# Layer 3 of a four-layer image kernel: GpSimd's additions kept back by a one-column copy, VectorE's taps divided anew among three units

## Chip, cores and metric

The kernel runs on one core of a Trainium2 chip. The metric is the device time of one execution in microseconds. Three executions of the kernel before took 12,790.3, 12,794.5 and 12,797.0 us.

## What is computed

The input is a float32 image batch of 4 x 48 x 256 x 256. Four layers follow each other; each normalises in groups, applies its function and adds the result to its input. Layers 0 and 3 are feed-forward layers with a spectral filter, layers 1 and 2 are scans over rows and columns. The change touches layer 3 alone:

```python
y = einsum('oc,bchw->bohw', w_in, x)          # 48 -> 288 channels
f = rfft2(8x8 patches of y) * fft_mask
y = irfft2(f)
y = conv 3x3, one filter per channel (w_dw)   # 288 channels
x1, x2 = split(y, 2)                          # 144 + 144
g = gelu(x1) * x2
out = einsum('oc,bchw->bohw', w_out, g)       # 144 -> 48
```

In layer 3 this function is applied to the normalised image, and the image is added to it.

## The kernel before

Layer 3 works on two pairs of images. A pair's 256 rows are cut into strips of 8 rows (RB); after the 32 strips of a pair comes one short step, the tail, for the last row. That makes 66 steps, 64 of them full strips.

The 288 channels of the 3x3 convolution are in three groups of image buffers: z_a0 and z_a1 (the halves x1 and x2 of the first 128 channels, for one image of the pair), z_b0 and z_b1 (the same for the other image), and z_m, which holds the 16 channels that are left over, for both images and both halves. The nine taps of the convolution are computed in three ways at once:

- **TensorE** does all of a0 and a1, and the lower half of the rows of b0 and b1, as products with small diagonal matrices (L1173, L1189). 288 such products make a *unit*. A step has three units: a0, a1 and b.
- **VectorE** does the upper half of the rows of b0 and b1. begin (L1232) has ScalarE write tap 0, and eight further taps follow, each a scalar_tensor_tensor over 128x1024 that reads an image and an accumulator in SBUF (L1237). The eight wait in the list due, and together hands them out one at a time while a unit runs. After the eighth tap of b0 comes ScalarE's gelu (L1239), after that of b1 a product of the two accumulators (L1241).
- **ScalarE and GpSimd** do z_m. narrow lays out 18 pieces of work in the list coming: nine taps times two halves of the rows. For a tap, ScalarE writes a product into part (L1263; three buffers), and GpSimd adds part to acc_m (L1264, 128x512). Tap 0 is ScalarE's alone (L1260). product takes one piece from the list, and its calls stand at chosen places of the step.

A step runs like this. Pixels of a0 are made from the spectra (products pp, L1133, and copies to z_a); then the second half of the spectra of this step (pz, L1095, with VectorE's L1098 and L1103) lies between the two pixel products of b0; then unit a0 runs. In it stands the gate of the previous step's z_m: gate_few finishes the list coming, then narrow_gate computes gelu on ScalarE (L1282, into a buffer gl) and the product on VectorE (L1285). Then the pixels of a1 are made and copied by VectorE (L1053, z_a), those of z_m follow, the previous step's output products run (po, L1300 and L1312), VectorE adds the input to them (L1324) and SyncE stores them. Then comes unit a1, with its gates (L1220) at the end. Then come the waves of the next step (pf, L1074), the pixels of b1 and the first half of the next step's spectra (L1095, L1098). Then unit b runs; at its end lower_gate has ScalarE compute a gelu (L1199) and VectorE two products (L1201).

All these PSUM tiles (pd, pp, pz, po, pt, pf) come from one pool of four buffers with the one tag w. The buffers gl come from a pool with two, as do the output rows xo.

The order on TensorE, VectorE, ScalarE and SyncE is that of the code. GpSimd is not in that list, and its order is left to the scheduler that builds the program:

```python
FIXED = {mybir.EngineType.PE, mybir.EngineType.DVE, mybir.EngineType.Activation}
...
st.enter_context(tc.manual_schedule(engines=FIXED | {mybir.EngineType.SP}))
```

The taps are handed out by this line of together, where t runs over the nine taps of a unit and k % 3 is 0 in unit a0:

```python
if due and (t in (0, 1, 3, 4, 6) or t == 7 and k % 3 == 0):
    due.pop(0)[1]()
```

Of the kernel before, what the change touches and what calls it, by code (L numbers as in the profile page):

```python
# [9 lines left out]
F32 = mybir.dt.float32  # L10
AF = mybir.ActivationFunctionType
ALU = mybir.AluOpType
# [21 lines left out]
class Net:  # L34
# [903 lines left out]
    def layer3(self, x, scs):  # L938
# [6 lines left out]
        nc, tc, W, H, NQ, HD = self.nc, self.tc, self.W, self.H, self.NQ, HID3  # L945
        NM, NR, WP, R2 = 128, HID3 - 128, W + 2, MM // W
        steps = [(p, s) for p in range(self.NP) for s in range(H // RB + 1)]
        tail = lambda step: step[1] == H // RB
        odd = lambda step: steps.index(step) % 2
        with ExitStack() as st:  # L950
            pool = lambda name, bufs, **k: st.enter_context(tc.tile_pool(name=name, bufs=bufs, **k))
            wp, inp, wz = pool("w3", 1), pool("in3", 1), pool("z3", 1)
            io, mid = pool("io3", 2), pool("mid3", 1)
            ps_w = pool("ps3w", 4, space=PSUM)
            st.enter_context(tc.manual_schedule(engines=FIXED | {mybir.EngineType.SP}))
            HR = RB // 2
# [79 lines left out]
            gated = {g: wz.tile([128, 4, MM], F32, name=f"g_{g}", tag=f"g_{g}") for g in "ab"}  # L1036
# [159 lines left out]
            def lower_gate(pds):  # L1196
                gl = io.tile([128, 2, MM], F32, name="gl", tag="gl")
                x1, x2 = (pd.rearrange("p k r w -> p k (r w)") for pd in pds)
                nc.scalar.activation(gl, x1, AF.Gelu)  # L1199
                for l in range(2):  # L1200
                    nc.vector.tensor_tensor(  # L1201
                        gated["b"][64:128, 2 * l : 2 * l + 2], gl[64 * l : 64 * l + 64],
                        x2[64 - 64 * l : 128 - 64 * l], ALU.mult,
                    )
# [5 lines left out]
            def curve(step, x1):  # L1210
                gl = io.tile([128, 2, MM], F32, name="gl", tag="gl")
                x1 = flat(step, x1)
                gl = gl[0 : x1.shape[0], 0 : x1.shape[1], 0 : x1.shape[2]]
                nc.scalar.activation(gl, x1, AF.Gelu)  # L1214
                return gl

            def gate(step, img, k0, gl, x2):
                to, x2 = gated[img], flat(step, x2)
                n, k, m = x2.shape
                nc.vector.tensor_tensor(to[0:n, k0 : k0 + k, 0:m], gl, x2, ALU.mult)  # L1220
# [3 lines left out]
            whole, full, due, begun = {}, set(), [], {}  # L1224
# [18 lines left out]

                due.extend(((step, half), lambda t=t: tap(t)) for t in range(1, 9))

            few, coming, curved = {}, [], [None]

            def narrow(step):


                n, rows = (64, 1) if tail(step) else (128, HR)
                at = lambda t: zt["m"][0:n, t // 3 : t // 3 + rows, t % 3 : t % 3 + W]
                acc = mid.tile([128, HR, W], F32, name="acc_m", tag="acc_m")
                few[step] = acc
                acc = acc[0:n, 0:rows]
                half = lambda ap, r: ap[:, R2 * r : min(R2 * r + R2, rows)]

                def tap(t, r):
                    if t == 0:
                        nc.scalar.activation(half(acc, r), half(at(0), r), AF.Identity, bias=none[0:n], scale=wd[0:n, 2, 0:1])  # L1260
                        return
                    part = mid.tile([128, R2, W], F32, name="part", tag="part", bufs=3)[0:n, 0 : min(R2, rows)]
                    nc.scalar.activation(part, half(at(t), r), AF.Identity, bias=none[0:n], scale=wd[0:n, 2, t : t + 1])  # L1263
                    nc.gpsimd.tensor_tensor(half(acc, r), half(acc, r), part, ALU.add)  # L1264

                halves = range(1 if tail(step) else 2)
                coming.extend(lambda t=t, r=r: tap(t, r) for t in range(9) for r in halves)

            def product(last=False):
                while coming:  # L1270
                    coming.pop(0)()
                    if not last:
                        return

            def narrow_gate(step, j0):
                if j0 == 0:
                    curved[0] = io.tile([128, HR, W], F32, name="gl", tag="gl")
                gl, acc = curved[0], few[step]
                for j0 in (j0,) if j0 == 0 or not tail(step) else ():
                    x1, x2 = slice(32 * j0, 32 * j0 + 32), slice(32 * j0 + 32, 32 * j0 + 64)  # L1280
                    rows = 1 if tail(step) else HR
                    nc.scalar.activation(gl[x2, 0:rows], acc[x1, 0:rows], AF.Gelu)  # L1282
                    for j in range(1 if tail(step) else 2):
                        to, r = slice(32 * (j0 + j), 32 * (j0 + j) + 32), slice(R2 * j, min(R2 * j + R2, rows))
                        nc.vector.tensor_tensor(acc[to, r], gl[x2, r], acc[x2, r], ALU.mult)  # L1285
# [58 lines left out]
            def unit(l, step, img):  # L1344


                n, blocks = steps.index(step), (2 * l, 2 * l + 1)
                pd = None
                if img == "b":
                    if not tail(step):  # L1350
                        if l == 0:
                            both[:] = [ps_w.tile([128, 2, R2, W], F32, name="pd", tag="w") for _ in range(2)]
                        yield from lower_taps(l, blocks, both)
                else:
                    pd = ps_w.tile([128, 2, R2, W], F32, name="pd", tag="w")
                    yield from taps(step, img, int(img[1]), blocks, pd)
                if img == "a0":
                    waiting[l] = curve(step, pd)
                    return
                assert n == 0 or steps[n - 1] in out  # L1360
                if img == "a1":
                    gate(step, "a", 2 * l, waiting[l], pd)
                elif l and not tail(step):
                    lower_gate(both)

            def together(k, aside):


                going = [unit(l, *units[l][k]) for l in range(2)]
                for t in range(9):  # L1370
                    for g in list(going):
                        if next(g, None) is None:
                            going.remove(g)
                    if t in aside:
                        aside[t]()
                    if due and (t in (0, 1, 3, 4, 6) or t == 7 and k % 3 == 0):
                        due.pop(0)[1]()
                for g in going:
                    assert next(g, None) is None
# [14 lines left out]
            def ready(n):  # L1394

                if fresh(n):
                    state["u"] = normed(steps[n])
# [15 lines left out]
            def spectra(n, k, part=slice(None)):  # L1413
                if fresh(n):
                    for q0, m in (cuts_rest if k else cuts)[part]:
                        spectrum(state["xf"], k, q0, m)

            def lower(n, half, q0, eng):
                if q0 == 0 and n:
                    drain(steps[n - 1], half)  # L1420
                pixels(steps[n], f"b{half}", q0, eng)
                if q0:
                    begin(steps[n], half)

            def gate_few(n, j0):
                if n >= 0:
                    product(True)
                    narrow_gate(steps[n], j0)

# [10 lines left out]
            for n, step in enumerate(steps):  # L1440
                pixels(step, "a0", 0, "AA")
                pixels(step, "a0", 8, "AA")
                product()
                spectra(n, 1, slice(0, 1))
                lower(n, 0, 0, "AA")
                spectra(n, 1, slice(1, 3))
                lower(n, 0, 8, "AA")
                spectra(n, 1, slice(3, None))
                product()
                gates = {4: lambda: gate_few(n - 1, 0), 6: lambda: gate_few(n - 1, 2)}  # L1450
                together(3 * n, {0: product, 1: product} | gates)

                pixels(step, "a1", 0, "DD")
                pixels(step, "a1", 8, "DD")
                pixels_rest(step, "AA")
                store(n - 1)
                narrow(step)
                if fresh(n + 2):
                    fetch(steps[n + 2])
                turn(n + 1, "AA")  # L1460
                together(3 * n + 1, {t: product for t in (0, 2, 3, 5, 6, 8)})

                wave(n + 1, "AA")
                product()
                lower(n, 1, 0, "AA")
                product()
                lower(n, 1, 8, "AA")
                product()
                spectra(n + 1, 0)
                together(3 * n + 2, {t: product for t in (0, 1, 5, 7, 8)} | {3: lambda: ready(n + 2)})  # L1470
            gate_few(S - 1, 0)
            gate_few(S - 1, 2)
            store(S - 1)
# [118 lines left out]
```

## Time and profile before

| | us |
|---|---|
| median of three runs | 12,794.5 |
| the profiled execution, its own time | 12,789.3 |
| its span | 12,787.5 |
| PE busy in the span | 11,859.6 (93%) |
| DVE busy | 7,870.3 (62%) |
| ACT busy | 4,692.9 (37%) |
| POOL busy | 3,177.0 (25%) |
| mean granted TensorE clock | 0.983 |

Layer 3 takes the last third of the span. In the stretch from 8700 to 12300 us, 3600 us long, the engines were busy for: PE 3286.87, DVE 2863.53, ACT 2270.23, POOL 1537.37 us.

PE is TensorE's matrix products, PEld its weight loads, DVE VectorE, ACT ScalarE, POOL GpSimd, SP SyncE. A line such as L1237 is a line of the kernel before. In a timeline, a row gives the start in us, the us that it and the like ones behind it took, the engine, the line, what is written and read, the shapes, how many there are, and in brackets how long the engine had been idle and for what. In the chain of waits, the work that ended last is followed back; "issue" is time in which the engine waited for nothing that the profile shows. Spans on POOL are rough.

### The profile page before, as it was taken

The page shows a single profiled execution, that of the slowest core. Times are in us where ns is not written, and L with a number is a line of the kernel's source. Part 1 is how long each engine was busy: PE and PEld are TensorE (multiplying, and loading weights), DVE is VectorE, ACT ScalarE, POOL GpSimd, SP SyncE. Part 2 cuts the span into 40 slices and gives each one's busy share as a digit, 9 for nine tenths or more (in the row PEclk, how much of TensorE's full clock was granted, in tenths as well). Part 3 has the DMA queues.
Part 4 walks back from the last instruction along what each step waited for, and adds up shares of the span by engine and source line. Part 5 has one row for each costly group of instructions (what it writes and reads, how often), then busy time and mean ns, then how long its engine had stood idle before and what let it go on. Part 6 is the DMA issues. An engine that isn't in the chain of part 4 may idle for free. (4 is left out here: it accounts for less than half of the span.)

```text
span 12787.5 us, 411497 instructions
## 1 busy us (share of the span) xinstructions
PE 11859.6 (93%) x190576; PEld 7852.5 (61%) x190576; DVE 7870.3 (62%) x11132; ACT 4692.9 (37%) x5761; POOL 3177.0 (25%) x2017
## 2 busy tenths in 40 slices
PE   2999899999999999999999999989999998999998
PEld 0333333336777777777777777766666666666665
DVE  6777777774333333663333335668888877777787
ACT  1444444442223200002233000026666666666665
POOL 0110111110000001550000003544444444444344
PEclk9999999999999999999999999999999999999999
DMA  7222222225765776988755977941111111111110
GB/s 178 59 57 57 54 59 57 59 54 97 156 136 150 176 153 139 217 203 157 151 141 150 178 150 169 228 96 28 28 28 28 25 25 30 23 28 28 28 28 21
DMA packets 1170307, 1223.68 MB, mean 96 GB/s; under 512 B 1027668, under 2 KB 1031756, under 8 KB 1107724
## 3 DMA queue, kind: packets, MB, share of 16 engines
q1 hardware_dynamic: 1066052, 623.85, 26.4%
q0 software_dynamic: 87488, 445.55, 12.1%
q10 hardware_dynamic: 15048, 127.96, 5.4%
q8 instruction: 1494, 24.48, 0.8%
q14 instruction: 225, 1.84, 0.1%
HBM read 699.79 MB, written 497.42 MB: 94 GB/s over the span
## 5 line engine op out<-in xcount | busy, mean ns | idle before, releaser
L684 PE MATMUL acc<-line,w_down 96*96 96x256 f32 x12240 | 2660.8, 379 | 14.6 <-ACT line L782 5.0
L1264 POOL TENSOR_TENSOR acc_m<-acc_m,part 128x512 f32<-128x512 f32 (+1 forms) x1040 | 1821.3, 1772 | 2433.7 <-ACT part L1263 2432.9
L684 PEld LDWEIGHTS acc<-line,w_down 96*96 96x96 f32 x12240 | 1989.1, 163 | 671.6 <-DVE line L826 11.5
L1237 DVE SCALAR_TENSOR_TENSOR acc<-z_b,wd,acc 128x1024 f32<-128x1024 f32 (+1 forms) x1056 | 1815.8, 1719 | 40.9 <-ACT acc L1232 11.8
L313 PE MATMUL pd<-main,diag 32*32 32x512 f32 x36864 | 1415.4, 617 | 76.4 <-issue 65.8
L1173 PE MATMUL pd<-z_a,diag 32*32 32x512 f32 x37152 | 1319.9, 596 | 46.2 <-issue 41.6
L684 PE MATMUL acc<-line,w_right 96*96 96x256 f32 x6120 | 1341.5, 380 | 21.4 <-DVE line L864 10.1
L684 PE MATMUL acc<-line,w_left 96*96 96x256 f32 x6120 | 1337.6, 379 | 9.8 <-DVE line L905 7.5
L350 DVE SCALAR_TENSOR_TENSOR acc<-rest,wd,acc 128x1024 f32<-128x1024 f32 x1024 | 1254.9, 1283 | 121.0 <-ACT acc L344 97.4
L684 PEld LDWEIGHTS acc<-line,w_right 96*96 96x96 f32 x6120 | 997.9, 163 | 353.3 <-DVE line L867 17.2
L684 PEld LDWEIGHTS acc<-line,w_left 96*96 96x96 f32 x6120 | 995.4, 163 | 338.8 <-DVE line L905 16.3
L1173 PEld LDWEIGHTS pd<-z_a,diag 32*32 32x32 f32 x37152 | 792.2, 103 | 476.3 <-issue 202.2
L124 ACT ACTIVATE nrm<-nrm 96x2 f32<-96x2 f32 (+1 forms) x7 | 1.4, 203 | 2793.5 <-DVE nrm L123 1423.8
L867 DVE SCALAR_TENSOR_TENSOR line<-acc,b_right,in 96x256 f32<-96x256 f32 x1020 | 489.3, 480 | 857.4 <-PE acc L684 849.6
L791 DVE TENSOR_TENSOR line<-acc,in 96x256 f32<-96x256 f32 x1020 | 429.1, 421 | 919.9 <-PE acc L684 914.9
L826 DVE SCALAR_TENSOR_TENSOR line<-acc,b_down,in 96x256 f32<-96x256 f32 x992 | 476.0, 480 | 830.5 <-PE acc L684 825.4
L313 PEld LDWEIGHTS pd<-main,diag 32*32 32x32 f32 x36864 | 501.3, 104 | 775.4 <-issue 659.3
L1098 DVE TENSOR_TENSOR z<-pz,mask 128x768 f32<-128x768 f32 (+2 forms) x640 | 628.8, 1005 | 499.3 <-PE pz L1095 497.1
L915 POOL TENSOR_TENSOR blk<-blk,line 96x1024 f32<-96x1024 f32 x248 | 705.3, 2873 | 606.7 <-DVE line L905 606.7
L833 ACT COPY blk<-line 96x1024 f32<-96x1024 f32 (+2 forms) x264 | 479.9, 1890 | 923.4 <-DVE line L826 760.2
L905 DVE SCALAR_TENSOR_TENSOR line<-acc,b_left,in 96x256 f32<-96x256 f32 x992 | 475.7, 480 | 529.4 <-PE acc L684 529.4
L1263 ACT ACTIVATE part<-z_m,none,wd 128x512 f32<-128x512 f32 (+1 forms) x1040 | 786.1, 803 | 6.2 <-POOL acc_m L1264 6.1
(167 smaller groups left out, 13663.6 us busy)
## 6 DMA issues: line engine op xcount, KB each, us to landing
blk<-x ACTq DMA_DIRECT2D x64, 1536.0 KB, 18.6
in<-x SPq DMA_DIRECT2D x248, 384.0 KB, 11.3
dn<-line POOLq DMA_DIRECT2D x124, 768.0 KB, 9.5
rt<-line POOLq DMA_DIRECT2D x124, 768.0 KB, 9.8
in<-rt SPq DMA_DIRECT2D x124, 768.0 KB, 12.6
in<-dn SPq DMA_DIRECT2D x120, 768.0 KB, 6.8
in<-up SPq DMA_DIRECT2D x240, 384.0 KB, 12.0
up<-blk POOLq DMA_DIRECT2D x56, 1536.0 KB, 14.3
```

The costliest lines, as they stand in the source:

```text
L313: nc.tensor.matmul(pd[32 * j : 32 * j + 32, i], diag[s, t, :], z[s, R2 * j + t // 3 : R2 * j + t // 3 + R2, t % 3 : t % 3 + W], start=(t = ...
L350: nc.vector.scalar_tensor_tensor(to, at(t, r), wd[:, 1, t : t + 1], to, ALU.mult, ALU.add)
L684: self.nc.tensor.matmul(acc, w[:, t, :], carry[:, :, t : t + m], start=(t == 0), stop=(t == 2))
L826: nc.vector.scalar_tensor_tensor(inner(line), acc, bd, new[r], ALU.add, ALU.add)
L833: nc.scalar.copy(blk[:, :, e, lo:hi, k // 2 : k // 2 + RH], inner(ln[:, e::2])[..., lo:hi].rearrange("p h i w -> p i w h"),)
L867: nc.vector.scalar_tensor_tensor(blocks(inner(line)), blocks(acc), br, new, ALU.add, ALU.add)
L915: (nc.vector if w0 == 0 else nc.gpsimd).tensor_tensor(part, part, inner(ln[:, f::2])[..., lo:hi].rearrange("p w i h -> p i h w"), ALU.add)
L1098: nc.vector.tensor_tensor(zs[k][:, q0 : q0 + n].rearrange("p q b c -> p b q c"), pz[:, :, :, 0:NM], mask[:, :, :, NM * k : NM * k + NM].to ...
L1173: nc.tensor.matmul(pd[32 * j : 32 * j + 32, i, 0:n, :], diag[s, half, t, :], zt[g][s, R2 * j + t // 3 : R2 * j + t // 3 + n, t % 3 : t % 3 ...
L1237: nc.vector.scalar_tensor_tensor(acc, at(t), wd[:, half, t : t + 1], acc, ALU.mult, ALU.add)
L1263: nc.scalar.activation(part, half(at(t), r), AF.Identity, bias=none[0:n], scale=wd[0:n, 2, t : t + 1])
L1264: nc.gpsimd.tensor_tensor(half(acc, r), half(acc, r), part, ALU.add)
```

## The change

The additions of GpSimd are put aside in a list held while hold is set, which it is from the start of unit a1 and, except in the tail, of unit b. At the end of the unit release calls a copy of one column into a small tile mark (from g_a after unit a1, from gl after unit b), and then the additions. product does nothing while three are held. The calls of product are moved: in unit a1 to t = 0 to 4 (six calls before, five after), in unit b to t = 0, 1, 2 (five before, three after), in unit a0 to t = 0, 1, 2 (two before, three after), and one more between the two pixel products of b0.

VectorE's taps are handed out four in unit a0 and six each in units a1 and b; before it was six, five and five. The buffer of narrow_gate is taken from the two buffers of xo instead of those of gl. The first half of the next step's spectra is divided: two of its four parts come between the two pixel products of b1.

```diff
@@ -1197,6 +1197,7 @@
                 gl = io.tile([128, 2, MM], F32, name="gl", tag="gl")
                 x1, x2 = (pd.rearrange("p k r w -> p k (r w)") for pd in pds)
                 nc.scalar.activation(gl, x1, AF.Gelu)
+                release(gl[:, 0, 0:1])
                 for l in range(2):
                     nc.vector.tensor_tensor(
                         gated["b"][64:128, 2 * l : 2 * l + 2], gl[64 * l : 64 * l + 64],
@@ -1243,7 +1244,15 @@
 
                 due.extend(((step, half), lambda t=t: tap(t)) for t in range(1, 9))
 
-            few, coming, curved = {}, [], [None]
+            few, coming, curved, hold, held = {}, [], [None], [False], []
+            mark = wp.tile([128, 1], F32, name="mark")
+
+            def release(sign):
+
+                nc.gpsimd.tensor_copy(mark, sign)
+                hold[0] = False
+                while held:
+                    held.pop(0)()
 
             def narrow(step):
 
@@ -1261,20 +1270,21 @@
                         return
                     part = mid.tile([128, R2, W], F32, name="part", tag="part", bufs=3)[0:n, 0 : min(R2, rows)]
                     nc.scalar.activation(part, half(at(t), r), AF.Identity, bias=none[0:n], scale=wd[0:n, 2, t : t + 1])
-                    nc.gpsimd.tensor_tensor(half(acc, r), half(acc, r), part, ALU.add)
+                    add = lambda: nc.gpsimd.tensor_tensor(half(acc, r), half(acc, r), part, ALU.add)
+                    held.append(add) if hold[0] else add()
 
                 halves = range(1 if tail(step) else 2)
                 coming.extend(lambda t=t, r=r: tap(t, r) for t in range(9) for r in halves)
 
             def product(last=False):
-                while coming:
+                while coming and len(held) < 3:
                     coming.pop(0)()
                     if not last:
                         return
 
             def narrow_gate(step, j0):
                 if j0 == 0:
-                    curved[0] = io.tile([128, HR, W], F32, name="gl", tag="gl")
+                    curved[0] = io.tile([128, HR, W], F32, name="gm", tag="xo")
                 gl, acc = curved[0], few[step]
                 for j0 in (j0,) if j0 == 0 or not tail(step) else ():
                     x1, x2 = slice(32 * j0, 32 * j0 + 32), slice(32 * j0 + 32, 32 * j0 + 64)
@@ -1360,6 +1370,8 @@
                 assert n == 0 or steps[n - 1] in out
                 if img == "a1":
                     gate(step, "a", 2 * l, waiting[l], pd)
+                    if l == 0:
+                        release(gated["a"][:, 0, 0:1])
                 elif l and not tail(step):
                     lower_gate(both)
 
@@ -1373,7 +1385,7 @@
                             going.remove(g)
                     if t in aside:
                         aside[t]()
-                    if due and (t in (0, 1, 3, 4, 6) or t == 7 and k % 3 == 0):
+                    if due and t in ((0, 2, 4, 6) if k % 3 == 0 else (0, 1, 3, 4, 6, 7)):
                         due.pop(0)[1]()
                 for g in going:
                     assert next(g, None) is None
@@ -1424,6 +1436,7 @@
 
             def gate_few(n, j0):
                 if n >= 0:
+                    assert not held and not hold[0]
                     product(True)
                     narrow_gate(steps[n], j0)
 
@@ -1443,12 +1456,13 @@
                 product()
                 spectra(n, 1, slice(0, 1))
                 lower(n, 0, 0, "AA")
+                product()
                 spectra(n, 1, slice(1, 3))
                 lower(n, 0, 8, "AA")
                 spectra(n, 1, slice(3, None))
                 product()
                 gates = {4: lambda: gate_few(n - 1, 0), 6: lambda: gate_few(n - 1, 2)}
-                together(3 * n, {0: product, 1: product} | gates)
+                together(3 * n, {0: product, 1: product, 2: product} | gates)
 
                 pixels(step, "a1", 0, "DD")
                 pixels(step, "a1", 8, "DD")
@@ -1458,16 +1472,19 @@
                 if fresh(n + 2):
                     fetch(steps[n + 2])
                 turn(n + 1, "AA")
-                together(3 * n + 1, {t: product for t in (0, 2, 3, 5, 6, 8)})
+                hold[0] = True
+                together(3 * n + 1, {t: product for t in range(5)})
 
                 wave(n + 1, "AA")
                 product()
                 lower(n, 1, 0, "AA")
                 product()
+                spectra(n + 1, 0, slice(0, 2))
                 lower(n, 1, 8, "AA")
                 product()
-                spectra(n + 1, 0)
-                together(3 * n + 2, {t: product for t in (0, 1, 5, 7, 8)} | {3: lambda: ready(n + 2)})
+                spectra(n + 1, 0, slice(2, None))
+                hold[0] = not tail(step)
+                together(3 * n + 2, {t: product for t in (0, 1, 2)} | {3: lambda: ready(n + 2)})
             gate_few(S - 1, 0)
             gate_few(S - 1, 2)
             store(S - 1)
```

## Prediction

> **What bounds the kernel now.** I read the page's table of 40 slices first: layer 3 begins near 8,490 us (first L1095 at 8494.1) and fills the last third of the span. Its work repeats once a strip: L1199 runs 64 times, 65.6 us apart in the median, so 1 us a strip is 64 us of the kernel. Everything the diff touches lies there. Then I read the chain of waits through two ordinary strips, to see which instruction is last at each hand-over (start, us, what):
> ```profile
> 9344.80 1.22 DVE g_b L1201
> ...
> 9355.36 1.86 DVE acc L1237
> 9357.23 0.02 issue
> 9357.25 2.19 DVE acc L1237
> ...
> 9361.68 1.22 DVE acc L1241
> ...
> 9367.13 1.03 ACT gl L1214
> ...
> 9370.14 5.38 PE po L1312 x64
> ...
> 9390.98 1.15 issue
> ...
> 9394.66 4.62 DVE z L1098 x4
> ...
> 9401.38 2.20 DVE acc L1237
> ...
> 9403.61 1.29 DVE acc L1237
> ```
> One strip is 9344.80 to 9409.36, from L1201 to L1201. The chain leaves VectorE for TensorE twice and comes back twice. TensorE is busy 91% of layer 3 (3286.87 of the 3600 us from 8700 to 12300), but it is not alone the bound: its waits say that it stands for VectorE after unit b, and for ScalarE, which stands for VectorE, before the output products (us in total, times, longest; 54 strips):
> ```profile
> PE pp L1133 <- DVE g_b L1201: 76.5, 53, 2.1
> PE pp L1133 <- issue: 74.5, 67, 1.9
> PE po L1300 <- ACT gl L1214: 63.2, 52, 2.0
> ```
> Last, the timeline of VectorE and of GpSimd in that strip:
> ```profile
> 9355.28 6.37 DVE L1237 SCALAR_TENSOR_TENSOR acc<-z_b,wd,acc 128x1024 f32<-128x1024 f32 x3
> ...
> 9367.05 2.61 DVE L1237 SCALAR_TENSOR_TENSOR acc<-z_b,wd,acc 128x1024 f32<-128x1024 f32 x2
> ...
> 9399.19 10.14 DVE L1237 SCALAR_TENSOR_TENSOR acc<-z_b,wd,acc 128x1024 f32<-128x1024 f32 x5
> ```
> ```profile
> 9354.85 5.72 POOL L1264 TENSOR_TENSOR acc_m<-acc_m,part 128x512 f32<-128x512 f32 x3 [6.69 <-ACT part L1263]
> ...
> 9387.74 1.29 POOL L1264 TENSOR_TENSOR acc_m<-acc_m,part 128x512 f32<-128x512 f32 x1 [0.81 <-ACT part L1263]
> ```
> A tap alone takes 1.30 us (2.61 for two), beside GpSimd's additions 2.19; an addition alone takes 1.28, beside taps up to 2.27. A met addition thus costs VectorE 0.91 us. Over layer 3 the tap's mean is 1.755 us, so some 8 of the 16 taps of a strip are met.
>
> Here the Trainium skill (SBUF — State Buffer, Who interferes with whom) has a rule: a VectorE instruction with two SBUF inputs and a GpSimd instruction that reads SBUF block each other for the whole instruction. A met tap would then last 1.30 + 1.28 = 2.58; the row has 2.19, so part of the two lies side by side. By the rule the five taps of unit b with four met additions would take 5 x 1.30 + 4 x 1.28 = 11.6 us; they take 10.14, so the row decides, and I count 0.91 for a meeting. What keeping the two apart could free is by the row 8 x 0.91 = 7.3 us of VectorE in a strip, by the rule 10.2: the rule speaks for a hold, if there is one.
>
> **Does the change hold the additions?** The copy into mark and the additions share no tile, and GpSimd is not among the engines whose order the code fixes. The order of the built program decides, and there the three additions that the code keeps back in unit a1 stand ahead of the copy that reads g_a, and the three of unit b ahead of the copy that reads gl. A queue in order cannot hold what stands before the wait. So I take it that **the additions run as soon as their part is there, as before**. Behind each copy stand only additions whose parts come later (after gl is ready at 9343.28 the next part starts at 9345.91, 2.6 us on; after unit a1 it is longer), so the copies hold up nobody. There is no row for a copy of one column on GpSimd; its memsets of 128x256 take 0.32 us, so between 0 and 0.3 us, in 36 us of GpSimd idle time per strip: nothing. What is left of the diff is a new division of taps and additions among the units, and that has a price.
>
> **Unit a0 (pixels of a0 to the output products).** Taken from the list of VectorE: 4 taps instead of 6. Added on GpSimd: 5 additions in a row after the spectra instead of 3 (third product, t = 0, 1, 2 and the last at t = 4), and one in the middle of the spectra, where VectorE reads PSUM and the mask and no tap is met: free. With 9344.80 as zero, the taps start at 10.5. Tap, tap and L1241 are now met by additions: 1.9 + 2.2 + 2.2, to 16.8 (before, L1241 came fourth and unmet). The third addition ends near 15.8, the fourth, met, at 15.8 + 2.26 = 18.0, the fifth alone 1.25 later, 19.3. Then nothing is hidden: L1282 1.06, two L1285 1.38, tap 1.30, two L1285 1.40, tap 1.30, to 25.75. The second copy L1053 z_a, whose PSUM buffer the second po needs (five L1312 run, the next starts at 9371.01, that is 26.2, just after that copy), ends at 26.95 instead of 26.04. That is **+0.9 us** (0.5 with the fourth addition half met, 1.4 with later ones).
> Taking gm from the xo buffers removes ScalarE's wait of 3.13 us before the second L1214 and so TensorE's 1.2 us (63.2/52) before L1300. But what is late next is that copy of z_a, which comes after the same taps, and L1300 itself is held by the later L1282 and L1214: at 23.8 instead of 23.4. Worth 0. The xo buffers are free by then: output DMAs land 3.5 us after issue.
>
> **Unit a1.** 6 taps instead of 5, three met additions: 6 x 1.3 + 3 x 0.91 = 10.5 us, beside TensorE's 11.0. VectorE had 1.47 us of idle before L1220, so 1.3 more just fits: **0** (up to +0.5 if it does not). One addition fewer after the gelu L1239: 0.
>
> **Between a1 and b.** The spectra of the next strip are halved around the second pixel product. TensorE's work is the same, but the first L1098 starts one product (1.05 us) earlier. The wait for issue comes 46 to 49 matmuls into L1133, within the first 64, so I leave it at its 1.2 us. After L1074: 1.05 + 1.2 + 3.84 + 1.05 = 7.1 us until the last spectrum is there, then 1.2 for the last L1098: 8.4 against 9.0 (4 x 1.2 behind the first product of pz before). **-0.6 us** (0 if another issue wait comes in; -1.9 if the wait goes altogether).
>
> **Unit b.** 6 taps instead of 5, the adds 4 (third product, t = 0, 1, 2) instead of 6. Only as many are met as before: of the six, one ran ahead of the taps and one half. 6 x 1.31 + 0.5 + 3 x 0.91 = 11.1 against 10.0 in the median strip, 10.14 here. L1201 follows the last tap by 0.03, and TensorE waits for L1201 already, so all of it counts: the extra tap, **+1.3 us** (+0.9 with one meeting fewer, +1.7 with one more). ScalarE's eight L1045 shift within unit b, whose gelu L1199 waits for TensorE: 0.
>
> **Sum.** 0.9 + 0 - 0.6 + 1.3 = +1.6 us a strip, of 65.6. Times 64: +104 us. The profiled execution took 12,789.3 us (span 12,787.5): 12,893. The three runs' median is 5 us higher; on that scale 12,899, and I say **12,900 us**.
>
> **Rivals.** About 0.2% (26 us, 0.4 us a strip) is what a measurement can tell from no change.
> *It holds after all* (faster). If the additions do wait for the unit's end, unit b has 6 taps of 1.31, 7.9 us, and VectorE is ready 2.2 us earlier. But L1201 needs the gelu L1199 too, which ends 1.4 us before VectorE is done now (L1199 9406.94 to 9407.96, L1201 at 9409.36). The saving stops at -1.4, and the spectra's -0.6 is lost in it; with a0's +0.9 that is -0.5 a strip, -32 us, some 12,762. It decides from the point where the copies stand ahead of the additions. For it: the code's order, and half the taps met now. Against: the order of the built program. 0.12.
> *It cancels* (no change): a0's fourth addition unmet, one meeting fewer in b, half the issue wait gone: 0.5 + 0.9 - 1.2 = +0.2, 12,807. 0.13.
> *VectorE runs late everywhere* (slower still): the sixth tap of a1 ends after TensorE's unit (+0.5), a0 +1.4, b +1.7, spectra 0: +3.6, 13,025. For it: DVE has little idle left in a1. Against: each is its upper end. 0.12.
> My forecast: 0.63.
>
> **Numbers.** Its own range is 12,830 to 12,960. To leave no more than 2 in 10 out, the range takes in the no-change case and much of the last: 12,790 to 12,975. Chances: faster 0.13, within 0.2% 0.13, slower 0.74.
>
> **What would show it.** In the new profile: a L1264 of mean 1.7 us or more and taps of 2.2 us still in a1 and b (if they are 1.3 throughout, it does hold and I am wrong); GpSimd's five additions after the spectra, with ScalarE's gelu L1282 some 19.3 us after L1201, not 15.8; TensorE's wait for L1201 at some 2.1 us a strip (TensorE is 0.9 later there, L1201 1.6), up from 1.4; no wait of L1214 for L1285; the issue wait in L1133 unchanged. The a0 and b terms are the ones that would sink the forecast.

## Result, and the profile after

The changed kernel takes 12,994 us (median of four runs, 12,977 to 13,008) where the kernel before takes 12,796 on the same chip: a ratio of 1.0153, 95% interval 1.014 to 1.0166. The forecast was slower, 12,900, in a range of 12,790 to 12,975; the loss is 198 us, 3.1 us a strip, and not the 1.6 that I had summed. The profiled execution has a span of 12,991.8 us, at a mean granted clock of 0.973 instead of 0.983.

GpSimd first. Its timeline in one strip of the changed kernel (L1252 is the copy into mark; the lines behind it have moved: L1273 is the old L1264, L1238 the old L1237, L1202 the old L1201, L1215 the old L1214, L1221 the old L1220, L1322 the old L1312):

```profile
9321.40 7.96 POOL L1273 TENSOR_TENSOR acc_m<-acc_m,part 128x512 f32<-128x512 f32 x4 [3.05 <-ACT part L1272]
9330.79 1.01 POOL L1252 COPY mark<-gl 128x1 f32<-128x1 f32 x1 [1.43 <-ACT gl L1199]
...
9346.05 9.17 POOL L1273 TENSOR_TENSOR acc_m<-acc_m,part 128x512 f32<-128x512 f32 x5 [4.96 <-ACT part L1272]
9372.67 6.36 POOL L1273 TENSOR_TENSOR acc_m<-acc_m,part 128x512 f32<-128x512 f32 x3 [17.45 <-ACT part L1272]
9381.31 0.18 POOL L1252 COPY mark<-g_a 128x1 f32<-128x1 f32 x1 [2.28 <-DVE g_a L1221]
```

The three additions of unit a1 end 2.3 us before the copy that should hold them, the four that run in unit b 1.4 us before theirs. Nothing is held, as the order of the program had said. The five additions in a row after the spectra are there too. The six taps of unit b, four of them met, take 11.6 us, those of unit a1 10.6:

```profile
9321.47 11.61 DVE L1238 SCALAR_TENSOR_TENSOR acc<-z_b,wd,acc 128x1024 f32<-128x1024 f32 x6
9333.11 2.46 DVE L1202 TENSOR_TENSOR g_b<-gl,pd 64x1024 f32<-64x1024 f32 x2
...
9369.54 10.57 DVE L1238 SCALAR_TENSOR_TENSOR acc<-z_b,wd,acc 128x1024 f32<-128x1024 f32 x6
9380.03 2.34 DVE L1221 TENSOR_TENSOR g_a<-gl,pd 128x1024 f32<-128x1024 f32 x2
```

What TensorE waits for, in the same stretch of 3600 us as before (us in total, times, longest):

```profile
PE pp L1133 <- DVE g_b L1202: 147.4, 51, 3.0
PE pp L1152 <- ACT gl L1215: 76.8, 51, 2.0
PE pp L1133 <- issue: 46.8, 49, 1.7
PE po L1322 <- DVE z_a L1053: 24.5, 42, 0.6
```

The wait for L1202 has doubled, from 1.4 to 2.9 us a time. What I had not looked for stands behind that wait. First the products of TensorE there in the changed kernel, then the same ones in the kernel before:

```profile
9335.71 1.99 PE L1133 MATMUL pp<-c_inv,z 64*64 64x64 f32 x64 [2.94 <-DVE g_b L1202]
9337.63 3.57 PE L1095 MATMUL pz<-wi,xf 48*128 48x160 f32 x24
9341.13 1.55 PE L1133 MATMUL pp<-c_inv,z 64*64 64x64 f32 x64
```
```profile
9347.40 1.16 PE L1133 MATMUL pp<-c_inv,z 64*64 64x64 f32 x64 [2.07 <-DVE g_b L1201]
9348.50 1.90 PE L1095 MATMUL pz<-wi,xf 48*128 48x160 f32 x24
9350.33 1.16 PE L1133 MATMUL pp<-c_inv,z 64*64 64x64 f32 x64
```

The same products take up to 1.9 times as long. The table by stretches gives the granted clock in them (PEclk; it, the DMA share and GB/s are the last three columns), again the changed kernel first:

```profile
9335.60:9344.00 8.40, 8.29 (x172) 7.80 (x174) 3.92 (x7) 3.06 (x6) 1.28 (x2) 0.62 0.01 2
```
```profile
9347.30:9353.50 6.20, 6.10 (x180) 5.67 (x180) 4.51 (x8) 3.09 (x5) 0.85 (x1) 1.00 0.01 3
```

After the longer wait TensorE is granted half its clock for a while. In the clock records of the traces, from 8,600 to 12,400 us, the half clock lasts 119 us before and 338 us after; there it comes in 36 pieces of 3.4 us, 24 of 6.8 and five of 10.2. Behind this one wait, counted up to 3 us past the first tap of a0, it lasts 58 us before and 266 after. At half clock 208 us more lose at most 104 us of work: an estimate of 1.9 us for each of the 55 strips in that stretch.

The strip by parts, from L1201 to L1201 (us). For each point I took its time after L1201 and the median over 60 full strips of the trace; a part is the difference of two such medians:

| part | before | after | forecast of the difference | measured |
|---|---|---|---|---|
| L1201 to the first tap of a0 | 10.52 | 12.08 | 0 | +1.56 |
| to the second copy of z_a | 15.58 | 16.49 | +0.9 | +0.91 |
| to the first L1074 | 17.70 | 17.57 | 0 | -0.13 |
| to the end of the last L1098 | 12.06 | 11.28 | -0.6 | -0.78 |
| to the next L1201 | 9.82 | 11.58 | +1.3 | +1.76 |
| strip | 65.68 | 69.00 | +1.6 | +3.32 |

### The profile page after: what moved, and what is told of

It reads as the page before. It is cut to its first block, busy times and chain, and to the rows that moved or that the text cites. A ratio compares the mean times of both kernels' runs of the same rounds, so it can differ in the third digit from the quotient of the medians.

```text
span 12991.8 us, 411994 instructions
## 1 busy us (share of the span) xinstructions
PE 11997.6 (92%) x190576; PEld 7955.2 (61%) x190576; DVE 7955.6 (61%) x11132; ACT 4706.3 (36%) x5761; POOL 3266.4 (25%) x2147
## 5 line engine op out<-in xcount | busy, mean ns | idle before, releaser
L1273 POOL TENSOR_TENSOR acc_m<-acc_m,part 128x512 f32<-128x512 f32 (+1 forms) x1040 | 1831.5, 1783 | 2286.9 <-ACT part L1272 2266.3
L1238 DVE SCALAR_TENSOR_TENSOR acc<-z_b,wd,acc 128x1024 f32<-128x1024 f32 (+1 forms) x1056 | 1836.4, 1739 | 39.0 <-ACT acc L1233 9.9
L1098 DVE TENSOR_TENSOR z<-pz,mask 128x768 f32<-128x768 f32 (+2 forms) x640 | 634.3, 1007 | 507.0 <-PE pz L1095 504.9
L1133 PE MATMUL pp<-c_inv,z 64*64 64x64 f32 x32768 | 644.7, 233 | 233.8 <-DVE g_b L1202 176.5
L1133 PEld LDWEIGHTS pp<-c_inv,z 64*64 64x64 f32 x32768 | 582.7, 146 | 388.7 <-issue 321.0
```

What stands on the lines that cost most here:

```text
L1098: nc.vector.tensor_tensor(zs[k][:, q0 : q0 + n].rearrange("p q b c -> p b q c"), pz[:, :, :, 0:NM], mask[:, :, :, NM * k : NM * k + NM].to ...
L1133: nc.tensor.matmul(pp[64 * c : 64 * c + 64, l, q, :], z[f, q0 + q, b, 64 * c : 64 * c + 64], self.inv1[f, :], start=True, stop=True,)
L1238: nc.vector.scalar_tensor_tensor(acc, at(t), wd[:, half, t : t + 1], acc, ALU.mult, ALU.add)
L1273: add = lambda: nc.gpsimd.tensor_tensor(half(acc, r), half(acc, r), part, ALU.add)
```

## Experiments

Theory: one term is missing from the sum. VectorE is late after unit b, TensorE's wait grows from 1.4 to 2.9 us on average, the granted clock halves, and the spectra that follow cost 1.5 us more. Rivals: the products after the wait are slow because of the extra piece of ScalarE's and GpSimd's work between the spectra; or the copies into mark cost something. Ratios are to the kernel before, run on the same chip; the times on different chips are some 20 us apart.

**1. No copies.** The line `nc.gpsimd.tensor_copy(mark, sign)` is taken out.

> The changed kernel without the two copies into mark (the lists are still filled and emptied). Theory: in the changed kernel the copies stand behind the additions that they should hold, so nothing changes: 12,994 within 20 us. Rival (the copies delay GpSimd and so VectorE): 30 us or more faster.

13,034 us, with the kernel before at 12,815 there: 1.0173 (1.015 to 1.0196). The time is 20 us above the range that I expected; the ratio's interval overlaps that of the changed kernel, and there is no gain. So the copies hold nothing, and no cost of theirs shows.

**2. The wait filled.** In the changed kernel, the first spectrum after unit b is computed three times into the same place:

```diff
-                for q in range(n):
+                for q in [*range(n)] * (3 if k and not q0 else 1):
```

> The changed kernel, with the twelve products of the first spectrum after unit b issued three times into the same place: 2.2 us of work for TensorE inside its wait of 2.9 us for L1202, same result. Theory (the wait drops TensorE's granted clock to half for the products that follow, 1.5 us a strip): half-clock time falls to that of the kernel before or less, and the time by 64 x 1.5 = 95 us, to about 12,900. Rival (the products after the wait are slow because of ScalarE's and GpSimd's extra work between the spectra): no gain, 12,994 to 13,030.

12,915 us, 1.0072 (1.0055 to 1.0089). More work for TensorE, and 0.8% less time. The products behind the wait, now of 1.3 us, are back at full speed:

```profile
9344.17 2.72 PE L1095 MATMUL pz<-wi,xf 48*128 48x160 f32 x36
9348.20 1.16 PE L1133 MATMUL pp<-c_inv,z 64*64 64x64 f32 x64 [1.32 <-DVE g_b L1202]
9349.29 1.90 PE L1095 MATMUL pz<-wi,xf 48*128 48x160 f32 x24
```

The half clock falls from 338 to 113 us, and behind this wait from 266 to none; the part from L1202 to the first tap falls from 12.08 to 10.48 us. The extra piece between the spectra is still there, so that rival is out. What remains against the 12,815 us there, 100 us, is the size of the prediction's sum (104).

**3. The division of the taps alone**, in the kernel before.

```diff
-                    if due and (t in (0, 1, 3, 4, 6) or t == 7 and k % 3 == 0):
+                    if due and t in ((0, 2, 4, 6) if k % 3 == 0 else (0, 1, 3, 4, 6, 7)):
```

> The kernel before with the taps alone divided 4, 6 and 6. Sum by the steps of the prediction: output products 1.6 us earlier (two taps fewer ahead of the copies of z_a, three additions as before), L1201 1.3 later after unit b, net -0.3 us a strip, 12,775, if the clock plays no part. Theory (clock): TensorE now waits 2.7 us for L1201, so up to 1.5 us a strip come on top: 12,840 to 12,880, with half-clock time near that of the changed kernel. Rival (extra work between the spectra, which is not here): 12,775.

13,014 us, 1.0154 (1.0139 to 1.0169): this one line costs as much as the whole change, and more than the 12,880 that I allowed it. The output products do come earlier (z_a 2.3 us), but L1201 comes 11.8 us after the spectra, not 9.8, TensorE waits 3.4 us on average, and L1201 to the first tap takes 13.6 us instead of 10.5. Half clock: 416 us.

```profile
PE pp L1133 <- DVE g_b L1201: 174.3, 51, 4.3
```

**4. The same with the wait filled**, by three and by six times the twelve products.

> The kernel before with the taps divided 4, 6 and 6 and with the first spectrum's twelve products issued three times after unit b. Theory (the division alone costs 0.3 us a strip, the clock 3.1): the strip goes from 69.0 us of the division alone to about 65.9, ratio to the kernel before 1.000 to 1.003. Rival (what the division costs is VectorE's lateness, and the clock only accompanies it): ratio stays at 1.010 or more.

1.0089 (1.0073 to 1.0105): missed. Three times left a wait of 2.1 us, 38 of 63 strips still slow, and 259 us of half clock. So the wait was not filled, and the run could not tell the two apart. With six:

> The kernel before with the taps divided 4, 6 and 6, the first spectrum's products now issued six times (three left TensorE a wait of 2.1 us and the slow products). Theory: with the wait filled, the strip of 67.85 us of the run with three loses its remaining 1.5 us: about 66.3, ratio 1.001 to 1.005. Rival (the repeated products help by something else, or the division costs by itself): 1.008 or more.

1.0046 (1.0033 to 1.006), in the range. Half clock 68 us, first tap at 10.7 us. Of the 1.54% that the division costs, 1.1 goes when the wait is filled, and with it all half clock behind that wait. The rest is the strip's +1.05 us: a0 -1.96, unit b +2.3 (a sixth tap and one addition more met), the others +0.7, in which the repeated products' own time is not told apart.

**5. The halved spectra alone**, in the kernel before (`spectra(n + 1, 0, slice(0, 2))` ahead of the second pixel product of b1, the rest after it).

> The kernel before with the next strip's spectra halved around the second pixel product of b1, alone. By the prediction's term: -0.6 us a strip, 38 us faster, 12,757; with the clock theory a little more, as TensorE's wait for L1201 shrinks from 1.4 to 0.8 us (half-clock time falls). Rival (the halving gives nothing, since unit b is bound elsewhere): 12,795.

12,932 us, 1.0092 (1.0077 to 1.0107): slower, against all that I had expected. The term itself is as forecast: L1074 to the last L1098 is 0.77 us shorter. But the taps of b now start when GpSimd's additions do, and all five are met:

```profile
9339.01 5.73 POOL L1264 TENSOR_TENSOR acc_m<-acc_m,part 128x512 f32<-128x512 f32 x3 [4.42 <-ACT part L1263]
9345.08 6.32 POOL L1264 TENSOR_TENSOR acc_m<-acc_m,part 128x512 f32<-128x512 f32 x3 [0.34 <-ACT part L1263]
```
```profile
9339.18 11.09 DVE L1237 SCALAR_TENSOR_TENSOR acc<-z_b,wd,acc 128x1024 f32<-128x1024 f32 x5
```

They took 10.14 before. So L1201 comes 1.32 us later after the spectra, TensorE waits 2.4 instead of 1.4 us on average, and the part to the first tap, with 309 us of half clock in the stretch, takes 1.67 more: -0.77 + 1.32 + 1.67, with +0.07 elsewhere, is the strip's +2.29. That the 1.67 is the clock is read from experiments 2 and 4; the wait was not filled in this kernel.

**6. The other buffer for narrow_gate alone**, in the kernel before (`tag="xo"`).

> The kernel before with the buffer of narrow_gate taken from those of xo, alone. By the prediction's step: worth 0, since the copies of z_a hold the second output tile as before: ratio 0.999 to 1.001, and no wait of L1214 for L1285. Rival (TensorE's wait of 1.2 us a strip before L1300 goes): ratio 0.994.

1.0002 (0.9992 to 1.0013): nothing. TensorE's wait went one place on: 63.2 us for L1214 before L1300 have gone, 60.2 us for the copies of z_a before L1312 have come, as the chain had it.

```profile
PE po L1312 <- DVE z_a L1053: 60.2, 53, 1.9
```

**7. The additions really held.** In the changed kernel GpSimd joins the engines whose order is that of the code.

```diff
-            st.enter_context(tc.manual_schedule(engines=FIXED | {mybir.EngineType.SP}))
+            st.enter_context(tc.manual_schedule(engines=FIXED | {mybir.EngineType.SP, mybir.EngineType.Pool}))
```

> The changed kernel with GpSimd among the engines whose order is that of the code, so that the additions do stand behind the copies into mark. Rival of the prediction, now tried: taps of units a1 and b at 1.3 us, L1202 right after the gelu L1199, TensorE's wait under 1 us, so no half clock; the five additions after the spectra stay (+0.9). From the strip of the run with repeated products (67.4) less 2.3: 65.1, ratio to the kernel before 0.995 to 0.998. If holding is of no use: 1.010 to 1.016, as the changed kernel.

12,759 us against 12,819, 0.9947 (0.993 to 0.9964): faster than both, and a little faster than expected. Now the copy stands first, and the additions behind it. In unit b VectorE is done before the gelu is, for which L1202 waits:

```profile
9355.53 0.18 POOL L1252 COPY mark<-gl 128x1 f32<-128x1 f32 x1 [8.06 <-ACT gl L1199]
9355.67 4.98 POOL L1273 TENSOR_TENSOR acc_m<-acc_m,part 128x512 f32<-128x512 f32 x4
9361.49 1.28 POOL L1273 TENSOR_TENSOR acc_m<-acc_m,part 128x512 f32<-128x512 f32 x1 [0.84 <-ACT part L1272]
9365.55 9.17 POOL L1273 TENSOR_TENSOR acc_m<-acc_m,part 128x512 f32<-128x512 f32 x5 [2.79 <-ACT part L1272]
```
```profile
9346.22 8.92 DVE L1238 SCALAR_TENSOR_TENSOR acc<-z_b,wd,acc 128x1024 f32<-128x1024 f32 x6
9355.50 2.45 DVE L1202 TENSOR_TENSOR g_b<-gl,pd 64x1024 f32<-64x1024 f32 x2 [0.35 <-ACT gl L1199]
```

The mean tap falls from 1.780 to 1.443 us, the last L1098 to L1202 from 11.58 to 9.20, and the half clock to 99 us, none of it behind L1202. The five additions after the spectra stay, and with them a0's 0.9 us. GpSimd's fixed order without the copies was not tried; that the copies hold is shown by the 8.06 us for which the copy waits with the additions behind it.

**8. Two pieces moved ahead as well.** One more product in the middle of each half of the spectra, two fewer in unit a0:

```diff
                 lower(n, 0, 0, "AA")
                 product()
+                product()
...
-                together(3 * n, {0: product, 1: product, 2: product} | gates)
+                together(3 * n, {0: product} | gates)
...
                 spectra(n + 1, 0, slice(0, 2))
+                product()
                 lower(n, 1, 8, "AA")
```

> As the run before this one, with one more piece of z_m's work in the middle of each half of the spectra (a0's and b1's) and two fewer in unit a0, so that three additions follow the spectra, not five. Theory (a0's term is the run of additions that the gelu of acc_m waits for): the output products start 2.8 us earlier than in the run before and some 2 us earlier than in the kernel before; strip about 62.4 us, ratio 0.983 to 0.987. Rival (TensorE or ScalarE bounds the strip then): 0.992 to 0.998.

12,569 us against 12,819, **0.9805 (0.979 to 0.982)**, 250 us less than the kernel before, the fastest of all, and faster than I had expected. Three additions follow the spectra, the taps of a0 to the second copy of z_a take 13.04 us, the strip 61.9. After unit b TensorE, not VectorE, is late, as in experiment 7: L1202 waits for the gelu.

```profile
9321.16 5.72 POOL L1273 TENSOR_TENSOR acc_m<-acc_m,part 128x512 f32<-128x512 f32 x3 [1.56 <-ACT part L1272]
```
```profile
9362.66 8.92 DVE L1238 SCALAR_TENSOR_TENSOR acc<-z_b,wd,acc 128x1024 f32<-128x1024 f32 x6
9371.94 2.45 DVE L1202 TENSOR_TENSOR g_b<-gl,pd 64x1024 f32<-64x1024 f32 x2 [0.35 <-ACT gl L1199]
```

**9 and 10. Its two halves taken away**: GpSimd's order left to the scheduler again, and the old division of taps.

> The fastest version so far (additions really held, two pieces of z_m's work moved ahead), but with GpSimd's order left to the scheduler as in the changed kernel, so that nothing is held. Theory: a0's part of the gain stays (3.4 us on the changed kernel's 69.0), the long wait for L1202 and the half clock stay too: strip about 65.7, ratio 0.997 to 1.004. Rival (moving the pieces is the whole gain, holding is worth little): 0.981 to 0.986.

1.004 (1.0029 to 1.0052), at the upper end. Without the hold 2.4% are lost; a0 keeps its gain (12.78 us), but b takes 11.6 us again, and the part to the first tap 13.43 us, 3 us more, with 372 us of half clock.

> The fastest version so far with the taps divided 6, 5 and 5 as in the kernel before. Theory: with the additions held, the two taps more in a0 put the copies of z_a 2.6 us later, and one fewer in b frees nothing, since L1202 waits for the gelu L1199 there: strip about 64.2, ratio 0.990 to 0.993. Rival (unit b with six taps is the bound, five are better): 0.975 to 0.980.

0.9918 (0.99 to 0.9936). The division 4, 6, 6 that costs 1.5% in the kernel before gains 1.1% once the additions are held: unit b takes 9.2 us with five taps or six, and a0 2.6 us less.

## Why the prediction was right in sign and wrong in size

- **That nothing is held** was right, in the trace and by experiments 1 and 7. The copy takes 0.18 us, but in unit b, where it meets VectorE, 1.01, not 0 to 0.3; experiment 1 finds no cost in it.
- **Unit a0, +0.9**: right (+0.91). The fourth and fifth addition set the gelu of acc_m, which starts 20.87 us after L1202; take off the 1.56 us by which the taps start late, and it is 19.3, as in experiment 2. The buffer of narrow_gate at 0 is right too (experiment 6).
- **Unit a1, 0**: right for TensorE (-0.13), though the taps do not quite fit: in the median they end 0.3 us after TensorE's unit (0.7 in the strip above), and the 1.47 us of idle time before L1221 are gone. TensorE hardly ever waits for it (1.1 us of the 3600).
- **The halved spectra, -0.6**: right by itself (-0.78), but not as a gain: taken alone it starts the taps on top of the additions. The wait for issue in L1133 did not stay as it was: it fell from 74.5 to 46.8 us in the stretch, and how much of the -0.78 is due to that is open.
- **Unit b, +1.3**: too small, +1.76. I had half a meeting too few: the taps start earlier there, so that all four additions fall on taps, which take some 2.2 us each.
- **The step that failed** is in unit b: "TensorE waits for L1201 already, so all of it counts: the extra tap". I took a wait to cost its own length (and had it at 2.1 us a strip, where it is 2.9), and left L1201 to the first tap of a0 at no change. That part measured +1.56 us a strip, 100 us of the 198. A wait of TensorE costs more than its length once the clock halves behind it; filling the wait (experiment 2) gave back just that part. The trace of before had the sign: its granted clock is below 1 in layer 3 here and there, and 14 of its 64 strips have the slow products, all behind waits of 1.3 us or more.
- **The hold as a rival**, 12,762, had its mechanism and nearly its size: 0.9947 where I had 0.9975. It is not what the change did, and I had left out that the hold also takes away the 58 us of half clock that stand behind this wait in the kernel before: the part to the first tap is 11.05 us on average there, 10.57 with the hold.
- **The last rival**, 13,025, lies nearer to the result, but that is luck: of its four upper ends only unit b's +1.7 came.

## What to carry to other kernels

An order that matters has to be carried by data or by a fixed order of the engine (only the second was tried here): a copy that nothing depends on can be passed, and the order of the built program shows whether it was. When VectorE and GpSimd both read SBUF, move the one that has slack to where the other reads PSUM; six taps with few met took less time here (8.9 us) than five with four met (10.1), and a step that merely shifts them can make more of them meet. When TensorE waits 2 us or longer in a loop, look at the granted clock of the stretch behind it before summing; a few repeated products in the wait tell whether it matters.

## What was not expected of the hardware

How long TensorE has to wait before its clock halves. In six traces (before, after, experiments 1, 3, 5 and 6) I took the wait ahead of the first pixel product of b0 and the time of the 64 + 24 products behind it, 2.99 us at full clock, and called a strip slow from 3.4 us. A column takes the waits within 0.25 us of its heading:

```
wait (us)      0.5   1.0   1.5   2.0   2.5   3.0   3.5   4.0
strips           9    29    58    57    80    93    14    25
slow, share   0.00  0.00  0.28  0.56  0.86  0.94  1.00  1.00
median (us)   2.99  2.99  2.99  4.49  4.61  4.59  4.88  5.48
```

The Trainium skill (TensorE: Matmul & The Clock Gate, Part 1: The HAM clock gate) has the clock fall to half after an idle window of some 3.4 us, in windows that run freely. The pieces of half clock here, 3.4, 6.8 and 10.2 us, agree with such windows, and the spread between 1.5 and 2.5 us would fit their running freely. But no wait of 3.4 us is needed: by that rule the waits of the changed kernel for L1202, 3.0 us at the longest, would cost no more than their length, and at 2 us more than half the strips are slow. So the measurement decides: in this loop the allowance is nearer 1 us than 3. The waits here stand among small products; whether one between large products needs as little was not measured.
